# A second level of Strassen in four of the seven gate and up products

## The chip, the cores and the metric

The kernel runs on one core of a Trainium2 chip. The metric is the device time of one execution in microseconds (us), as a median of several runs. The engines are TensorE (PE in the profile; PEld is its weight loading, which has a row of its own), VectorE (DVE), ScalarE (ACT), GpSimd (POOL) and SyncE (SP), which here only issues transfers. Each engine works through its own instructions in program order, and waits where one needs what another engine has not finished.

## What is computed

A transformer block in f32, on 8 batches of 512 rows with 512 features. An attention half comes first, with a residual; the change touches it at one place only. The feed-forward half follows:

```
x = fwht(x * SU_ug) / 64                      # Hadamard transform over 512 features
x_up   = x @ W_up.T   * (Wscale_ug[:2048] * 64)
x_gate = x @ W_gate.T * (Wscale_ug[2048:] * 64)
x = silu(x_gate) * x_up                       # 2048 features
x = fwht(x * SU_dp) / 64
x = x @ W_down.T * (Wscale_dp * 64)           # back to 512
```

before it the rows are normalised, and after it they are normalised again and added to the residual. The kernel folds the second Hadamard transform into the down weights during the attention half (the tensor `wdd` in DRAM).

## The kernel before, in words

The feed-forward half is written out in program order, by hand. **Batches** are taken in four pairs, p = 0 to 3. The 2048 features are 16 blocks of 128, taken in eight **feature pairs**, i = 0 to 7: blocks i and i + 8. A **unit** (p, i, what) makes the gate ("g") or the up ("u") of one feature pair for one batch pair; the loop at the end runs through 64 of them, gate and up in turn, and its index is `u`.

A unit is a product of a weight block of 2 x 2 sub-blocks (two feature blocks by two halves of the 512 inputs) with an input of 2 x 2 (two halves of the inputs by two batches). It is done by Strassen's method (in Winograd's form) with **seven products** in place of eight. A product is two f32 matmuls of 128 x 128 weights on 512 columns, accumulated into one PSUM bank (`product`, L968). The seven are issued in the order 1, 2, 6, 5, 7, 3, 4. The weight sums S1 to S4 that they need are made by GpSimd in the first batch pair (`combine`, L146 to L149), stored to DRAM (`keep_unit`) and read back for p > 0 (`load_unit`, from SP, two units ahead). The input differences T1 to T4 are made once in each batch pair by VectorE (`operand`, L234).

`seven` takes the products out of PSUM: products 1 and 5 by a ScalarE copy (m1, m5), the others by a VectorE add onto an earlier sum. GpSimd makes c22 = u3 + m5 (L1013) and adds m5 to c12 (L1015). The last sum, u3 (L1017), is written in place: it adds product 4 to the u3 that GpSimd's c22 reads. The four results are c11, c12, u3 and c22, each 128 features by the 512 rows of a batch. `use` applies the sigmoid (ScalarE), and scales and multiplies (VectorE `scalar_tensor_tensor`, L994 for gate, L999 for up). Four PSUM banks rotate among all products (`ubank`); four others hold the sums of the down product.

`down` issues four matmuls of one feature block for the down product of one batch; it is called twice in each unit, at the filler before product 4 and after the unit, and does nothing where no block is ready. The down weights `wd` are loaded once and stay. `finish` ends a batch (scale, statistics, normalise, residual, store). `in_step` prepares a row block of the next batch pair: `in_flip` transposes it and `in_had` multiplies it by the Hadamard matrix and does the last two levels on GpSimd.

Before the loop the last batch of the attention half is finished: four times a scaling (L926), an add (L927) and a store (L928) on GpSimd. In the first unit the filler (before product 4) has the statistics of two input rows, whose shifts are on VectorE ahead of u3g.

Of the kernel before, what the change touches and what calls it, by code (L numbers as in the profile page):

```python
# [33 lines left out]
def sandwich_kernel(  # L34
# [91 lines left out]
    def load_unit(p, i, what):  # L126
        u = units.index((p, i, what))
        pool, tag = (xpool, "x") if u % 3 == 0 else (xt_p, "xT")
        t = pool.tile([P, NT, D], F32, tag=tag, name=f"w_{p}_{i}_{what}")
        w = t.rearrange("p t d -> p (t d)").rearrange("p (s k m) -> p s k m", k=2, m=P)  # L130
        wt[p, i, what] = w
        if p > 0:
            nc.sync.dma_start(
                out=w[:, 0:7].rearrange("p s k m -> p (s k m)"), in_=wsd[i, what]
            )
            return
        for h in range(2):
            nc.sync.dma_start(
                out=w[:, 2 * h : 2 * h + 2].rearrange("p s k m -> p (s k) m"),
                in_=wsrc[what][:, ts(i + h * NH, P)].rearrange("(k p) m -> p k m", p=P),  # L140
            )
# [8 lines left out]

    def keep_unit(i, what):
        wsd[i, what] = dram.tile([P, 7 * 2 * P], F32, name=f"wsd_{i}_{what}", tag=f"wsd{i}{what}")
        nc.sync.dma_start(
            out=wsd[i, what], in_=wt[0, i, what][:, 0:7].rearrange("p s k m -> p (s k m)")
        )
# [65 lines left out]
    ops = {}  # L221

    def operand(p, k):

        b11, b21 = xb[2 * p][:, 0:2], xb[2 * p][:, 2:4]
        b12, b22 = xb[2 * p + 1][:, 0:2], xb[2 * p + 1][:, 2:4]
        if k == 0:
            ops[p] = {"B11": b11, "B21": b21, "B22": b22}
        o = ops[p]
        if k % 2 == 0:  # L230
            o["home"] = qkv.tile([P, NT, D], F32, tag="v", name=f"T{k + 1}_{p}")
        o[f"T{k + 1}"] = o["home"][:, 2 * (k % 2) : 2 * (k % 2) + 2]
        a, b = [(b12, b11), (b22, o.get("T1")), (b22, b12), (b21, o.get("T2"))][k]
        nc.vector.tensor_sub(o[f"T{k + 1}"], a, b)  # L234
# [4 lines left out]
    with ExitStack() as actx:  # L239
# [684 lines left out]
        for qc in range(NT):  # L924
            y, rs, sh = ys.pop((b, qc))
            nc.gpsimd.tensor_scalar(y, y, rs[:, 0:1], sh[:, 0:1], ALU.mult, ALU.add)  # L926
            nc.gpsimd.tensor_add(y, xr[b, qc], y)  # L927
            nc.gpsimd.dma_start(out=x1d[b][ts(qc, P), :], in_=y)  # L928
# [20 lines left out]
    y0 = [fs.tile([P, D], F32, tag=f"fy{t}", name=f"fy_0_{t}") for t in range(NT)]  # L949
    r0 = [fs.tile([P, D], F32, tag=f"xres{t}", name=f"xres_0_{t}") for t in range(2)]  # L950
    psy0 = [ps_y.tile([P, D], F32, tag=f"y{t}", name=f"psy_0_{t}") for t in range(NT)]
    ubank("u0")
    wd = fw.tile([P, NI, D], F32, name="wd")

    def wd_load(i):
        for f in (i, i + NH):
            nc.sync.dma_start(out=wd[:, f, :], in_=wdd[:, ts(f, D)])
# [6 lines left out]
    def product(p, i, what, n, slot, b):  # L964
        w, rhs = wt[p, i, what], ops[p][b]
        ps = ubank(f"{what}{n}_{p}_{i}")
        for k in range(2):
            nc.tensor.matmul(  # L968
                ps, lhsT=w[:, slot, k, :], rhs=rhs[:, k, :], start=k == 0, stop=k == 1
            )  # L970
        return ps

# [8 lines left out]
    def seven(p, i, what, filler):  # L981

        def temp(n):
            return fs.tile([P, S], F32, tag=n, name=f"{n}{what}_{p}_{i}")

        def use(c, b, half):
            f = i + half * NH
            if what == "g":  # L990
                wsg = pv[:, C_WSG + f : C_WSG + f + 1]
                s = fs.tile([P, S], F32, tag="sig", name=f"s_{b}_{f}", bufs=5)
                nc.scalar.activation(s, c, AF.Sigmoid, scale=wsg)
                nc.vector.scalar_tensor_tensor(s, c, wsg, s, ALU.mult, ALU.mult)  # L994
                gs[b, f] = s
            else:
                home = free.pop(0)
                g = fs.tile([P, S], F32, tag=f"g{home}", name=f"g_{b}_{f}")
                nc.vector.scalar_tensor_tensor(  # L999
                    g, c, wsu[:, f : f + 1], gs.pop((b, f)), ALU.mult, ALU.mult  # L1000
                )
                waiting[b].append((f, g, home, now[0]))

        bA, bB = 2 * p, 2 * p + 1
        m1, m5 = temp("m1"), temp("m5")
        c11, u2, c12, u3, c22 = (temp(n) for n in ("c11", "u2", "c12", "u3", "c22"))
        nc.scalar.copy(m1, product(p, i, what, 1, A11, "B11"))  # L1007
        nc.vector.tensor_add(c11, product(p, i, what, 2, A12, "B21"), m1)
        nc.vector.tensor_add(u2, product(p, i, what, 6, S2, "T2"), m1)
        use(c11, bA, 0)  # L1010
        nc.scalar.copy(m5, product(p, i, what, 5, S1, "T1"))
        nc.vector.tensor_add(u3, product(p, i, what, 7, S3, "T3"), u2)  # L1012
        nc.gpsimd.tensor_add(c22, u3, m5)  # L1013
        nc.vector.tensor_add(c12, product(p, i, what, 3, S4, "B22"), u2)
        nc.gpsimd.tensor_add(c12, c12, m5)  # L1015
        filler()
        nc.vector.tensor_add(u3, product(p, i, what, 4, A22, "T4"), u3)  # L1017
        use(c22, bB, 1)
        use(c12, bB, 0)
        use(u3, bA, 1)  # L1020

# [3 lines left out]
    def down():  # L1025

        b = turn_of[0]
        if b == NB - 1 or not waiting[b] or waiting[b][0][3] >= now[0]:
            return
# [6 lines left out]
        for t in range(NT):  # L1036
            nc.tensor.matmul(  # L1037
                ys_[t], lhsT=g[:, ts(t, P)], rhs=wd[:, f, :], start=n == 0, stop=n == NI - 1
            )
        free.append(home)  # L1040
        psy[b] = n + 1, ys_
        if n == NI - 1:
            turn_of[0] += 1
            finish(b, ys_)

    def finish(b, ps):

        y = y0 if b == 0 else [
            fs.tile([P, D], F32, tag=f"fy{t}", name=f"fy_{b}_{t}") for t in range(NT)
        ]  # L1050
        for t in range(NT):
            nc.vector.tensor_mul(y[t], ps[t], wsdp_bc)

        def norms():
            mv = stat.tile([P, NT, 2], F32, tag="mvo", name=f"mvo_{b}", bufs=2)
            r = []
            for t in range(NT):
                r.append(
                    r0[t] if b == 0 and t < 2
                    else fs.tile([P, D], F32, tag=f"xres{t}", name=f"xres_{b}_{t}")  # L1060
                )
                nc.sync.dma_start(out=r[t], in_=x1d[b][ts(t, P), :])
                bn(mv[:, t, :], y[t], f"o{b}_{t}")
            rs = inverse_std(mv, NT, f"o{b}")

            def close():
                sh = shift_of(mv, rs, NT, f"o{b}")
                for t in range(NT):
                    nc.scalar.activation(
                        y[t], y[t], AF.Identity, bias=sh[:, t : t + 1], scale=rs[:, t : t + 1]  # L1070
                    )
                    nc.gpsimd.tensor_add(y[t], r[t], y[t])
                    nc.sync.dma_start(out=out[b, ts(t, P), :], in_=y[t])

            ends.append(close)

        ends.append(norms)
# [6 lines left out]
    CUTS = [0, 1, 2, 3, 5, 6, 8, 9, 10, 11, 12, 13, 14, 15, 16, 16, 16]  # L1084
    FIRST_CUTS = [0, 0, 1, 2, 3, 5, 6, 8, 9, 10, 11, 12, 13, 14, 15, 16, 16]
    first = 2 * NT
    wd_load(0)
    wd_load(1)
    for u, (p, i, what) in enumerate(units):
        slot = u % (2 * NH)  # L1090
        last = slot == 2 * NH - 1
        cuts = CUTS if p else FIRST_CUTS
# [3 lines left out]
        if p == 0 and u + 1 < 2 * NH:  # L1096
            combine(*units[u + 1][1:])

        def filler():
            down()  # L1100
            proceed()
            if u == 0:
                in_stats(first)
                in_stats(first + 1)
                in_shift(first)
                in_shift(first + 1)
                in_norm(first)
            if 0 < u < 4:
                wd_load(2 * u)
                wd_load(2 * u + 1)  # L1110
            if p + 1 < NP:
                for s in range(cuts[slot], cuts[slot + 1]):
                    in_step(2 * NT * (p + 1) + s // 2, s % 2, len(rows))
                if last:
                    operand(p + 1, 0)
                    operand(p + 1, 1)

        seven(p, i, what, filler)
        if p == 0:
            keep_unit(i, what)  # L1120
        if last and p + 1 < NP:
            operand(p + 1, 2)
            operand(p + 1, 3)
        down()


    b = NB - 1
    blocks = [(f, g) for f, g, _, _ in waiting[b]]

    def down_rows(ps, t, lo, hi):  # L1130
        for n in range(lo, hi):
            f, g = blocks[n]
            nc.tensor.matmul(  # L1133
                ps, lhsT=g[:, ts(t, P)], rhs=wd[:, f, :], start=n == 0, stop=n == NI - 1
            )

    def end_rows(ps, t, eng):
        y = fs.tile([P, D], F32, tag=f"fy{t}", name=f"fy_{b}_{t}")
# [18 lines left out]
    for t in range(NT):  # L1157
        rest.append(fs.tile([P, D], F32, tag=f"xres{t}", name=f"xres_{b}_{t}"))
# [71 lines left out]
```

## Time and profile before

| | us |
|---|---|
| median of three runs | 2205.27 |
| lowest and highest | 2205.2, 2208.29 |
| the profiled execution | 2205.19 |
| its span, from the first to the last instruction | 2203.4 |
| first product of the feed-forward half | at 945.97 |

The granted TensorE clock is 0.997 of full speed on average over the span. Busy time by stretch (us of the span):

| stretch | PE | DVE | ACT | POOL | PE clock |
|---|---|---|---|---|---|
| 960 to 970 | 5.80 | 3.91 | 3.12 | 9.34 | 0.79 |
| 970 to 980 | 10.00 | 7.44 | 1.88 | 4.71 | 0.87 |
| 1200 to 1300 | 100.00 | 49.28 | 20.52 | 33.76 | 1.00 |
| 1500 to 1600 | 100.00 | 48.15 | 18.24 | 30.11 | 1.00 |
| 1900 to 2000 | 100.00 | 31.70 | 14.26 | 13.96 | 1.00 |

A page of the profile gives busy time by engine, the span in 40 equal slices, the chain of work that ended last, and the groups of instructions. In a group or timeline row, "out<-in" are the tiles by the program's names, then their shapes; the bracket is the idle time of the engine before it and who ended it. An f32 matmul shows as two passes, each with its weight load. Matmul passes overlap in the records, so the mean length of one is longer than the distance from one to the next.

### The profile page before, as it was taken

What the parts mean: (1) busy time and instruction counts of PE and PEld (TensorE: products, weight loads), DVE (VectorE), ACT (ScalarE), POOL (GpSimd) and SP (SyncE); (2) the same over time, 40 slices, a digit from 0 to 9 for tenths busy, and PEclk for the clock granted to TensorE, in tenths of its full rate; (3) what the DMA queues carried; (4) which work ended last, traced back from release to release, by engine and by line L of the source; (5) the groups of instructions that cost most, each with busy time, mean ns of one, the idle gap of its engine ahead of it and who ended that gap; (6) DMA issues with size and microseconds to landing.
All of it is one profiled execution on the core that took longest, in us unless ns stands there. A gap on an engine that the chain in (4) does not pass through costs nothing.

```text
span 2203.4 us, 22074 instructions
## 1 busy us (share of the span) xinstructions
PE 2151.6 (98%) x7993; PEld 868.4 (39%) x8000; DVE 1196.7 (54%) x1659; ACT 690.5 (31%) x958; POOL 1108.5 (50%) x1161
## 2 busy tenths in 40 slices
PE   8999999999999999989999999999999999999998
PEld 3323333333333332334444444444444444444443
DVE  5687768686868676365445533534434435334322
ACT  3444555555555545522211211211211211212101
POOL 4686978787878789655544332321422311212102
PEclk9999999999999999999999999999999999999999
DMA  3112111121212022343233211212212111211201
GB/s 116 39 21 59 44 44 54 40 58 40 59 40 58 21 73 62 94 139 129 88 105 115 98 43 55 98 55 74 78 39 74 70 50 69 70 46 68 78 0 58
DMA packets 141005, 144.40 MB, mean 66 GB/s; under 512 B 83152, under 2 KB 100688, under 8 KB 140896
## 3 DMA queue, kind: packets, MB, share of 16 engines
q1 hardware_dynamic: 140544, 141.91, 20.7%
q8 instruction: 63, 1.03, 0.2%
q0 software_dynamic: 352, 1.08, 0.1%
q14 instruction: 46, 0.38, 0.1%
HBM read 106.79 MB, written 35.91 MB: 65 GB/s over the span
## 4 chain that ended last, share of the span: by engine, by line
PE 78%; POOL 9%; DVE 8%; issue 2%; ACT 2%; DMA 1%; SPq 0%; POOLq 0%; DVEq 0%; ACTq 0%
PE psy L1037 17%; PE u L968 17%; PE g L968 17%; POOL p L576 4%; PE s L513 3%; PE ps_y L643 3%; PE t L559 3%; PE ops L588 3%; DVE nm L521 3%; PE psz L1133 2%; PE ps_k L424 2%; PE t L550 1%; PE ps_cq L392 1%; PE fxh L209 1%; POOL y L675 1%
## 5 line engine op out<-in xcount | busy, mean ns | idle before, releaser
L521 DVE TENSOR_REDUCE nm<-s 128x2 f32<-128x1024 f32 x256 | 300.8, 1217 | 206.9 <-PE s L513 206.8
L1037 PE MATMUL psy<-wd,g 128*128 128x512 f32 x896 | 402.6, 592 | 0.0
L576 POOL TENSOR_TENSOR p<-p,p 128x512 f32<-128x512 f32 x244 | 325.7, 1365 | 27.0 <-PE ops L588 19.3
L570 ACT ACTIVATE p<-t 128x1024 f32<-128x1024 f32 x256 | 248.2, 1021 | 104.0 <-PE t L559 104.0
L1037 PEld LDWEIGHTS psy<-wd,g 128*128 128x128 f32 x896 | 170.2, 190 | 214.3 <-issue 214.3
L968 PE MATMUL u<-T,w_u 128*128 128x512 f32 x512 | 232.9, 598 | 4.2 <-DVE u3g L1017 4.2
L968 PE MATMUL g<-T,w_g 128*128 128x512 f32 x512 | 230.2, 592 | 0.0
L1013 POOL TENSOR_TENSOR c22u<-u3u,m5u 128x512 f32<-128x512 f32 x32 | 40.6, 1268 | 369.0 <-DVE u3u L1012 369.0
L1013 POOL TENSOR_TENSOR c22g<-u3g,m5g 128x512 f32<-128x512 f32 x32 | 40.6, 1268 | 315.2 <-DVE u3g L1012 315.1
L968 PE MATMUL g<-xb,w_g 128*128 128x512 f32 x384 | 175.3, 592 | 1.2 <-issue 1.2
L968 PE MATMUL u<-xb,w_u 128*128 128x512 f32 x384 | 175.2, 592 | 0.0
L513 PE MATMUL s<-kT,qT 32*128 32x512 f32 x1024 | 156.9, 640 | 1.6 <-DVE nm L521 1.6
L968 PEld LDWEIGHTS u<-T,w_u 128*128 128x128 f32 x512 | 97.5, 192 | 124.7 <-issue 118.2
L559 PE MATMUL t<-qT,kT 32*128 32x512 f32 x1024 | 142.9, 597 | 0.0
L968 PEld LDWEIGHTS g<-T,w_g 128*128 128x128 f32 x512 | 96.3, 190 | 116.2 <-issue 114.1
L588 PE MATMUL ops<-p,v 128*32 128x512 f32 x1024 | 136.8, 605 | 0.0
L424 PE MATMUL ps_k<-xT,wkr_sb 128*128 128x512 f32 x256 | 118.9, 608 | 0.8
L643 PE MATMUL ps_y<-wo_sb,oT 128*128 128x512 f32 x256 | 115.8, 593 | 1.0 <-DVE oT L638 0.6
L968 PEld LDWEIGHTS g<-xb,w_g 128*128 128x128 f32 x384 | 72.9, 190 | 93.4 <-issue 90.5
L968 PEld LDWEIGHTS u<-xb,w_u 128*128 128x128 f32 x384 | 73.0, 190 | 91.8 <-issue 88.7
L1007 ACT COPY m1g<-g 128x512 f32<-128x512 f32 x32 | 18.8, 586 | 254.2 <-PE g L968 217.6
L550 PE MATMUL t<-brow,ones_b 32*128 32x512 bf16 x512 | 68.5, 383 | 12.3 <-DVE nm L521 9.7
(181 smaller groups left out, 2842.9 us busy)
## 6 DMA issues: line engine op xcount, KB each, us to landing
w_g<-wsd_g SPq DMA_DIRECT2D x24, 896.0 KB, 4.5
w_u<-wsd_u SPq DMA_DIRECT2D x24, 896.0 KB, 4.6
xr<-in_x SPq DMA_DIRECT2D x32, 256.0 KB, 2.7
xin<-x1d SPq DMA_DIRECT2D x32, 256.0 KB, 2.8
xres<-x1d SPq DMA_DIRECT2D x32, 256.0 KB, 5.5
out<-fy SPq DMA_DIRECT2D x32, 256.0 KB, 2.2
rec<-rd SPq DMA_DIRECT2D x124, 64.0 KB, 2.0
x<-in_x SPq DMA_DIRECT2D x7, 1024.0 KB, 5.4
```

Source lines behind the costliest of these rows:

```text
L424: nc.tensor.matmul(ps, lhsT=wkr_sb[:, k, ts(g, P)], rhs=xT[b][:, k, :], start=(k == 0), stop=(k == NK - 1),)
L513: nc.tensor.matmul(sp[j // 2][:, j % 2, :], lhsT=qT[b][rows, g, ts(qc, P)], rhs=kT[b][rows, g, :], start=True, stop=True,)
L521: nc.vector.tensor_reduce(nms[n][:, qc, 2 * h : 2 * h + 2], sp[h], AX.X, ALU.max, negate=True)
L550: nc.tensor.matmul(sp[j // 2][:, j % 2, :], lhsT=ones_b[rows, :], rhs=brow[n][rows].rearrange("p t q -> p (t q)"), start=True, stop=False,)
L559: nc.tensor.matmul(sp[j // 2][:, j % 2, :], lhsT=kT[b][rows, g, ts(c, P)], rhs=qT[b][rows, g, :], start=False, stop=True,)
L570: nc.scalar.activation(pt[n, c, h], sp[h], AF.Exp)
L576: nc.gpsimd.tensor_add(into, into, pt[n, c, j // 2][:, j % 2, :])
L588: nc.tensor.matmul(o_ps[n][j * DH : (j + 1) * DH, :], lhsT=vv[b][:, c, ds(g * P + j * DH, DH)], rhs=pt[n, c, j // 2][:, j % 2, :], start=( ...
L643: nc.tensor.matmul(ps, lhsT=oT[b][:, k, ts(qc, P)], rhs=wo_sb[:, k, :], start=False, stop=(k == NK - 1),)
L968: nc.tensor.matmul(ps, lhsT=w[:, slot, k, :], rhs=rhs[:, k, :], start=k == 0, stop=k == 1)
L1013: nc.gpsimd.tensor_add(c22, u3, m5)
L1037: nc.tensor.matmul(ys_[t], lhsT=g[:, ts(t, P)], rhs=wd[:, f, :], start=n == 0, stop=n == NI - 1)
```

## The change

Four of the seven products, 1, 5, 7 and 3, are now made for gate and up together. The gate's and the up's two matmuls of such a product are again a 2 x 2 by 2 x 2 block product: (gate, up) by the two halves of K in the weights, the two halves of K by the two halves of the 512 columns in the input. `deep` does it with seven matmuls of 128 x 128 weights on 256 columns, each into a bank of its own. This holds for i > 0 in the second batch pair and for all i in the third and fourth (`deep_pair`), 23 feature pairs in all; products 2, 6 and 4 stay as they were. The gate unit makes the four deep products, and the up unit finds its parts of them ready in `held` (tiles h1, h5, h7, h3):

```diff
+    def deep(p, i, n, gate, up, parts):
...
+        lhs = {
+            1: wg[:, slot, 0], 2: wg[:, slot, 1], 6: s[:, 1], 5: s[:, 0],
+            7: wu[:, slot, 0], 3: s[:, 2], 4: wu[:, slot, 1],
+        }
+        rhs = {
+            1: x_[:, 0, :HS], 2: x_[:, 1, :HS], 6: t[:, 1], 5: t[:, 0],
+            7: x_[:, 0, HS:], 3: x_[:, 1, HS:], 4: t[:, 2],
+        }
...
+        m1, m5, u2, u3 = (temp(m) for m in ("m1", "m5", "u2", "u3"))
+        nc.scalar.copy(m1, small(1))
+        nc.vector.tensor_add(gate[:, :HS], small(2), m1)
+        part()
+        nc.vector.tensor_add(u2, small(6), m1)
+        nc.scalar.copy(m5, small(5))
+        part()
+        nc.vector.tensor_add(u3, small(7), u2)
+        nc.gpsimd.tensor_add(up[:, HS:], u3, m5)
+        nc.vector.tensor_add(gate[:, HS:], small(3), u2)
+        nc.gpsimd.tensor_add(gate[:, HS:], gate[:, HS:], m5)
+        part()
+        nc.vector.tensor_add(up[:, :HS], small(4), u3)
+        while parts:
+            part()
```

A `part` is one of the four matmuls of a down product, put between the small ones of deep products 1, 5 and 3 (3 only for i > 0); deep product 7 has none. In a deep unit the sums of the upper level are arranged so:

```diff
+        m1 = get(1, "m1", down_parts() if what == "g" else ())
+        if what == "g":
+            catch_up()
+        nc.vector.tensor_add(c11, product(p, i, what, 2), m1)
...
+        scaling = use(c11, bA, 0)
+        early()
+        m5 = get(5, "m5", down_parts() if what == "g" else ())
+        nc.vector.tensor_add(u2, product(p, i, what, 6), m1)
+        scaling()
+        u3 = get(7, "u3")
+        nc.gpsimd.tensor_add(u3, u3, u2)
         nc.gpsimd.tensor_add(c22, u3, m5)
+        nc.gpsimd.tensor_add(m5, m5, u2)
+        middle()
+        c12 = get(3, "c12", down_parts() if what == "g" and i > 0 else ())
         nc.gpsimd.tensor_add(c12, c12, m5)
         filler()
+        nc.vector.tensor_add(u3, product(p, i, what, 4), u3)
+        hook(4)
+        late.append(use(c22, bB, 1))
+        late.append(use(c12, bB, 0))
+        late.append(use(u3, bA, 1))
```

`early` and `middle` hold the steps of the next batch pair's rows and the ends of a batch; `catch_up` issues the scalings that the unit before left in `late`. Units that are not deep keep their seven products, but put three of their scalings off in the same way.

What the deep products need:

```diff
+    def deep_operand(p, n):
+        tt[p, n] = fs.tile([P, 3, HS], F32, tag=f"tt{n}", name=f"tt{n}_{p}")
+        x_, t = ops[p][DEEP[n]], tt[p, n]
+        nc.vector.tensor_sub(t[:, 0], x_[:, 0, HS:], x_[:, 0, :HS])
+        nc.vector.tensor_sub(t[:, 1], x_[:, 1, HS:], t[:, 0])
+        nc.vector.tensor_sub(t[:, 2], x_[:, 1, :HS], t[:, 1])
+    def deep_last(p, n):
+        x_ = ops[p][DEEP[n]]
+        nc.vector.tensor_sub(x_[:, 0, HS:], x_[:, 1, HS:], x_[:, 0, HS:])
+    def deep_weights(i):
...
+        nc.vector.tensor_add(t[:, 0], wu[:, 0:8:2, 0], wu[:, 0:8:2, 1])
+        nc.vector.tensor_sub(s3[i], wg[:, 0:8:2, 0], wu[:, 0:8:2, 0])
+        nc.vector.tensor_sub(t[:, 1], t[:, 0], wg[:, 0:8:2, 0])
+        nc.vector.tensor_sub(t[:, 2], wg[:, 0:8:2, 1], t[:, 1])
+    def deep_load(p, i):
+        w2[i] = fs.tile([P, 3, 4, P], F32, tag="w2", name=f"w2_{p}_{i}")
+        nc.sync.dma_start(out=w2[i].rearrange("p a b m -> p (a b m)"), in_=w2d[i])
```

The weight sums of the second level, `w2`, are made by VectorE in the gate units of the first batch pair, stored, and read back in one buffer at each up unit before a deep pair, behind the load of the up weights on SP. The stored up weights hold the fourth sum `s3` in place of one of their parts; feature pair 0 keeps its plain up weights too ("raw"), since p = 1, i = 0 is not deep.

To make room, the down weights no longer stay: each down product reads a tile of 256 KB, four of which rotate, loaded from `wdd` after the down product that set its buffer free. The last batch's are loaded into buffers of inputs and weights that are done with. `finish` is cut into four steps in place of two, with two residual tiles.

At the start, the four scalings of the last attention rows go from GpSimd to VectorE, and the statistics of two input rows from the first unit to the second:

```diff
-            nc.gpsimd.tensor_scalar(y, y, rs[:, 0:1], sh[:, 0:1], ALU.mult, ALU.add)
+            nc.vector.tensor_scalar(y, y, rs[:, 0:1], sh[:, 0:1], ALU.mult, ALU.add)
...
-            if u == 0:
+        def middle():
+            if u == 1:
                 in_stats(first)
                 in_stats(first + 1)
...
+        if u == 1:
+            in_shift(first)
+            in_shift(first + 1)
+            in_norm(first)
```

## Prediction

> **What bounds the kernel now.** I read four views in this order: the page's busy rows and its slices, the groups of instructions kept apart by shape, the timeline of the stretch in which the feed-forward half starts, and a close timeline of TensorE. The page first:
>
> ```profile
> PE 2151.6 (98%) x7993; PEld 868.4 (39%) x8000; DVE 1196.7 (54%) x1659; ACT 690.5 (31%) x958; POOL 1108.5 (50%) x1161
> PE   8999999999999999989999999999999999999998
> PEld 3323333333333332334444444444444444444443
> DVE  5687768686868676365445533534434435334322
> POOL 4686978787878789655544332321422311212102
> PEclk9999999999999999999999999999999999999999
> ```
>
> From slice 18 on (the span is 2203.4 us, a slice 55 us) TensorE is full, at full clock, while VectorE is at three to five tenths and GpSimd falls from five to one or two. In the last three whole stretches of 100 us (1800 to 2100) TensorE is busy for 100.00 of each, VectorE for 44.9, 31.7 and 38.5, GpSimd for 21.0, 14.0 and 18.8. So the second half is a stream of matmuls, and its length is the number of passes times the pitch of a pass.
>
> The pitch cannot be taken from the mean in the group rows (592 ns), since passes overlap. It is in the close timeline (start, us, engine, line):
>
> ```profile
> 1531.29 0.19 PEld L1037 LDWEIGHTS psy<-wd,g 128*128 128x128 f32 x1 [0.24 <-issue]
> 1531.72 0.14 PEld L200 LDWEIGHTS fxt<-ident,xin 128*128 128x128 f32 x1 [0.24 <-issue]
> 1532.15 0.60 PE L200 MATMUL fxt<-ident,xin 128*128 128x128 f32 x4
> 1532.15 0.36 PEld L200 LDWEIGHTS fxt<-ident,xin 128*128 128x128 f32 x3 [0.29 <-issue]
> 1532.48 0.30 PEld L968 LDWEIGHTS g<-T,w_g 128*128 128x128 f32 x2
> 1532.58 1.88 PE L968 MATMUL g<-T,w_g 128*128 128x512 f32 x4
> ```
>
> Weight loads in front of 512-column passes start every 0.43 us. At the start of the half, 12 passes that begin at 949.48 are followed by the next group at 954.63: 5.15 us, so a pass is 0.4292 us, and an f32 matmul, which is two passes, 0.858 us. The same lines show the short end: four transposes of 128 columns in 0.60 us, the last of them 0.273 long, are 0.109 us apart, although each has a weight load of 0.14 us; and two ordinary weight loads (0.19 us each) fit into 0.30 us.
>
> The third thing is the start of the feed-forward half:
>
> ```profile
> 958.06 3.60 PE L968 MATMUL u<-xb,w_u 128*128 128x512 f32 x8
> 961.50 1.88 PE L968 MATMUL u<-T,w_u 128*128 128x512 f32 x4
> 967.58 4.64 PE L968 MATMUL u<-T,w_u 128*128 128x512 f32 x5 [4.20 <-DVE u3g L1017]
> ```
>
> TensorE waits 4.20 us for a PSUM bank, and its granted clock then falls to 0.79 and 0.87 in the next two stretches of 10 us: the chain gives 7.87 us to 12 passes from 967.58 that need 5.15 at full clock. This place costs 4.20 + 2.72 = 6.9 us.
>
> **Removed and added on TensorE.** In 23 of the 32 feature pairs (7 of the second batch pair, 8 each of the third and fourth) the products 1, 5, 7 and 3 of gate and up, four f32 matmuls of 512 columns, become seven of 256 columns. Before: 4 x 0.858 = 3.434 us. A 256-column pass is in no row. Lower end: half of 0.4292 is 0.2146 us; with the fixed 2.5 ns of each pass that the page named below gives, 0.2158. Upper end: the weight load sets the pitch, 0.19 us plus a hand-over that no row shows; with 0.05 us it is 0.24. The transposes, 0.109 us apart under loads of 0.14, and the two loads of 0.19 in 0.30 say that loads follow each other at about 0.11 us, so I take 0.2158. Seven small matmuls are then 14 x 0.2158 = 3.02 us, 0.41 us less, and 92 products give **-38.0 us** (at 0.24: -7 us).
>
> Here a rule speaks against the change. The Trainium skill, "TensorE: Matmul & The Clock Gate", section on packing small matmuls, says that a weight load overlaps with running matmuls only where their row groups differ. All loads here use all 128 rows. By the rule a product would cost 8 x (0.429 + 0.19) = 4.95 us before and 14 x (0.216 + 0.19) = 5.68 after, and 92 of them +67 us. The row decides: 896 loads of 0.19 us of the down products stand under passes that come every 0.429 us. The load lies beside the pass before it, and 0.19 is still less than 0.216.
>
> **VectorE, ScalarE, GpSimd.** A small product leaves PSUM by a half-width add or copy. From 692 ns for 512 elements (L1014) and 1217 ns for 1024 (L521) a 256-element one is about 0.43 us (estimate), a ScalarE copy about 0.37 (0.586 for 512, 1.021 for 1024). A deep pair has on VectorE 20 half adds (8.6 us) and 6 whole ones (4.2) where 10 whole ones were (6.9); with eight scalings of 0.74 to 1.02 us (6.9 in all) it rises from 13.8 to 19.7 us. GpSimd had four adds of 1.27 (5.1 us) and gets eight of these and eight half adds of 0.73 (16 us, and 3.4 more where an input row is transformed). TensorE needs for such a pair 28 x 0.858 - 1.65 + 3.5 x 4 x 0.858 = 34.4 us. All fits beside it.
>
> The order within it matters more. The added waits are for banks: four rotate, and each small product fills half of one, so that they turn twice as fast. Deep product 7 is the tightest, since no down product lies between its parts. Counted from the end of product 6: its sum starts on VectorE 0.26 us later (the lag between the last column and the reader in the trace) and ends at 0.95, the scaling that is queued next at 1.7 to 1.9, the first half add at 2.05 to 2.35, and part 6 of 7 wants that bank at 2.15. So 0 to 0.2 us a pair. In the up unit the last sum waits until GpSimd has read its operand: product 6 ends at 3.4, GpSimd is through with two adds at about 8.3 (9.4 with an input row in front of it), and product 4 ends at 8.6 (9.5). Behind that sum on VectorE stand the first adds of the next gate unit, and TensorE has 2.2 us of banks in hand. It just fits.
>
> A second rule bears on this: the Trainium skill, "SBUF — State Buffer", section on the two sides of ports, has VectorE instructions with two SBUF inputs and GpSimd's exclude each other for whole instructions. The row agrees in part: the scaling of c12u behind GpSimd's add has a median of 1.21 us, that of c11u 0.744, so a collision costs about 0.46. By the rule each of eight scalings could wait out a GpSimd add of 1.27, +10 us a pair and VectorE at 30 of 34.4 us; by the row +3.7 us and 23. I take the row. It adds a little to the waits above.
>
> At the turn to the next batch pair the operand differences (1.22 us each), the twelve half-width ones and the four last ones come in bursts on VectorE; the banks lend about 2 us, and I count 1 to 1.5 us twice. I put all stalls of this part at **+4 us** (0 to 15).
>
> **Transfers, all on SP.** The down weights come by 112 loads of 256 KB (2.2 to 5 us to land in the trace for that size, three down products of lead, over 20 us): hidden. The weight sums (768 KB) have one buffer, free when deep product 3 is done, and stand on SP behind the next up weights (896 KB, 4.6 us), which wait for the end of the gate unit. Both have landed some 7.5 us after it (estimate: 4.6 us and 0.79 MB at the 270 GB/s that follow from 896 KB in 4.6 us and 256 KB, the stores to out, in 2.2). The third part of the next deep product 1 wants the sums 1.72 + 1.72 + 3.43 + 1.72 + 1.72 = 10.3 us after it. Hidden by 2.8 us; without that cover, 23 times the lateness. In the first batch pair VectorE makes the sums (four adds of 0.61 to 1.2 us beside a pair of 36 us) and SP stores them: covered by the down products and product 4, 5.2 us.
>
> **The start.** The chain there is GpSimd: four times a scaling (0.77), an add (1.27) and an issue (0.6 and gaps) up to 962.15, then c22g and c12g, then the inverse deviations of two input rows, whose shifts stand on VectorE in front of u3g. The change takes the scalings to VectorE (four of about 0.6 us, in front of c11g, whose bank is wanted 2 us later), and the two rows' statistics to the next unit. GpSimd then ends c22g about 961, u3g about 961.7 (962.5 behind the four weight-sum adds), and TensorE wants the bank at 963.2. The scalings now stand behind the sums of the next unit; product 4 of the up unit may wait 0.4 us for u2u. **-6.4 us** (0 to -6.9).
>
> **Sum.** Of the profiled execution's 2205.19 us (span 2203.4; the median of the runs is 2205.27): -38.0 - 6.4 + 4 = -40.4, that is 2165 us. The tail, 10 us from the last matmul to the last store, stays.
>
> **The rivals.**
> 1. VectorE and GpSimd in lock, or the weight sums' transfer, cost 0.5 to 1.2 us more in every deep pair: +12 to +28 us, 2177 to 2193. For it: GpSimd's work triples, and three places above fit by less than 1 us or hang on one queue. Against it: none of these engines is busy for over 70% of the pair.
> 2. Weight loads set the pitch of half passes at 0.24 us: -7 - 6.4 + 4, 2196 us. The transposes speak against it.
> 3. Slower: the same mechanism in the small products with a pitch above 0.25 us, from which on seven halves with the start's gain cost what four wholes do. At 0.28 (load 0.19 and 0.09 for the hand-over) a product is 3.92 us, +45 us in all, 2205 + 45 - 6 + 4 = 2248 us. Against it: the 0.109 us of the transposes, in which a load of 0.14 was not waited out.
> 4. Fewer stalls than I count, none at all: 2160 to 2161 us. It belongs to the forecast's own range.
>
> That the change does not happen can be left out: the changed program issues 644 matmuls of 256 columns in place of 368 of 512.
>
> **How the numbers follow.** Forecast (2158 to 2174) 0.64; rival 1 0.22; rival 2 0.06; rival 3 0.05; between them and no change 0.03. The range 2157 to 2185 takes the forecast and the lower half of rival 1. A measurement can tell 0.2%, 4.4 us, from no change: faster 0.93, same 0.02, slower 0.05.
>
> **What would show it.** Weight loads of L1071 0.216 us apart (right) or 0.24 and more (rivals 2, 3). TensorE solid from 946 to the end with no wait of over 0.5 us in the deep pairs; waits of L1071 on the half adds, or of the sums on GpSimd, each of 23 pairs, are rival 1. No 4.2 us gap near 963 and a clock of 1.00 there. It would be wrong if a wait turned up in the first batch pair, whose order changes too.

## The result, and the profile after

The changed kernel takes 2174.26 us (median of four runs, 2172.91 to 2177.87) against 2206.78 for the kernel before on the same chip: a ratio of 0.9855, with a 95% interval of 0.9838 to 0.9872. The profiled execution took 2173.1 us, 32.1 less than the one before; the forecast was 40 less. One profile further down fell in a slower state of the chip, at a granted clock of 0.946 (2242.51 us): no stretch is read from it, and that kernel was run a second time.

The page of the changed kernel, busy rows and slices:

```profile
span 2171.3 us, 24623 instructions
PE 2115.1 (97%) x8552; PEld 971.1 (45%) x8552; DVE 1360.4 (63%) x2111; ACT 701.9 (32%) x1050; POOL 1352.1 (62%) x1433
PE   7999999999999999999999999999999999999998
DVE  6686768686868676465655755657555557455432
POOL 4686878787878879754554266464565644444542
PEclk9999999999999999999999999999999999999999
```

TensorE stays full from slice 17 on, with less to do. VectorE is mostly at five to seven tenths there, GpSimd at four to six. The small products are the rows of L1071, read here in the close timeline of an undisturbed stretch of the fourth batch pair, with a row of their weight loads (PEld) from one of the third (start, us, engine, line):

```profile
1971.50 1.88 PE L1050 MATMUL g<-T,w_g 128*128 128x512 f32 x4
1973.21 1.03 PE L1071 MATMUL d<-T,w_g 128*128 128x256 f32 x4
1974.08 1.03 PE L1071 MATMUL d<-tt,w 128*128 128x256 f32 x4
1974.94 0.38 PE L1071 MATMUL d<-T,w_u 128*128 128x256 f32 x1
...
1560.91 0.84 PEld L1071 LDWEIGHTS d<-tt,w 128*128 128x128 f32 x4
```

Four passes of 512 columns take 1.71 us (1971.50 to 1973.21), eight of 256 take 1.73 (1973.21 to 1974.94): 0.216 us a pass. Four weight loads of 0.19 us take 0.84 us from the start of the first to the end of the last, so they start 0.217 us apart, at the pace of the passes.

**A measure for the feed-forward half.** Programs with the same attention half reach their first feed-forward product anywhere between 944.65 and 950.31 us (more on this in the last section), so the profiles are compared from that product to the end of the last matmul pass. It lies 7.3 us before the end of the span in all of them; the sums below take 7.4 throughout, which shifts every half by 0.1 us and changes no difference. Before: 2203.4 - 7.4 - 945.97 = 1250.0 us. After: 2171.3 - 7.4 - 944.75 = 1219.1 us. The change saves 30.9 us there; the other 1.2 us of the profiled executions lie ahead of it.

**Where TensorE still waits.** I went through its timeline and took, for each group of passes, the distance to the next group less its passes times their pitch. These are the places of 0.25 us and more: the start of the half (2.96 us), the first unit of the second batch pair (0.87), and the two turns to the third and the fourth pair (4.25 and 5.13 us). Then come two waits for the load of the weight sums (0.46 and 0.30), and seven gaps of 0.36 us (0.25 and 0.11) in deep products 7 and 3. Of the 5.13 us of the second turn, 1.7 are no wait: behind its first wait the granted clock is 0.50 from 1813.25 to 1816.66. The start and the first turn in TensorE's timeline:

```profile
964.95 3.70 PE L1050 MATMUL u<-T,w_u 128*128 128x512 f32 x8 [2.80 <-DVE u3g L1169]
...
1507.26 0.70 PE L1071 MATMUL d<-xb,w_u 128*128 128x256 f32 x2 [2.74 <-DVE h L1193]
...
1514.73 1.12 PE L1217 MATMUL psy<-wd,g 128*128 128x512 f32 x2 [1.18 <-DVE g L1142]
```

The bracket says who ended the wait: the last sum of a unit (u3g, or h in the up unit), which frees a PSUM bank, and a scaling whose result is a down product's weight. What held the first two is in VectorE's timeline, first ahead of u3g, then ahead of h; two rows of GpSimd's stand behind it, the first and the last of its four sums at the turn:

```profile
955.93 2.06 DVE L991 TENSOR_TENSOR w<-w_u 128x512 f32<-128x512 f32 x1
957.91 4.13 DVE L992 TENSOR_TENSOR s<-w_g,w_u 128x512 f32<-128x512 f32 x1
961.96 1.21 DVE L993 TENSOR_TENSOR w<-w,w_g 128x512 f32<-128x512 f32 x1
963.20 1.09 DVE L994 TENSOR_TENSOR w<-w_g,w 128x512 f32<-128x512 f32 x1
964.22 0.68 DVE L1169 TENSOR_TENSOR u3g<-g,u3g 128x512 f32<-128x512 f32 x1
...
1499.44 0.42 DVE L976 TENSOR_TENSOR tt<-T 128x256 f32<-128x256 f32 x1
1499.89 1.37 DVE L977 TENSOR_TENSOR tt<-T,tt 128x256 f32<-128x256 f32 x1
1501.29 1.37 DVE L978 TENSOR_TENSOR tt<-T,tt 128x256 f32<-128x256 f32 x1
1502.59 1.48 DVE L976 TENSOR_TENSOR tt<-T 128x256 f32<-128x256 f32 x1
1504.10 1.37 DVE L977 TENSOR_TENSOR tt<-T,tt 128x256 f32<-128x256 f32 x1
1505.51 0.42 DVE L978 TENSOR_TENSOR tt<-T,tt 128x256 f32<-128x256 f32 x1
1505.85 0.42 DVE L983 TENSOR_TENSOR xb<-xb 128x256 f32<-128x256 f32 x1
1506.18 0.42 DVE L983 TENSOR_TENSOR T<-T 128x256 f32<-128x256 f32 x1
1506.52 0.68 DVE L1193 TENSOR_TENSOR h<-u,h 128x512 f32<-128x512 f32 x1
...
1498.94 2.04 POOL L1186 TENSOR_TENSOR h<-h,u2u 128x512 f32<-128x512 f32 x1 [5.70 <-DVE u2u L1183]
1503.86 1.32 POOL L1191 TENSOR_TENSOR h<-h,h 128x512 f32<-128x512 f32 x1
```

The same instruction takes 0.42 us or 1.37. From 1498.94 to 1505.18 GpSimd does the four sums of the up unit; each stretched difference ends 0.28 or 0.29 us after one of them (1501.26 after 1500.98, 1505.47 after 1505.18), so it looks like waiting for the sum to end. At 956.15 to 961.48 GpSimd adds a residual row, then c22g, c12g and the first weight sum of the next unit. The four sums of L991 to L994 take 8.5 us.

### The profile page after: what moved, and what is told of

Its sections match the earlier page's. It is cut to its first block, busy times and chain, and to the rows that moved or that the text cites. A ratio compares the mean times of both kernels' runs of the same rounds, so it can differ in the third digit from the quotient of the medians.

```text
span 2171.3 us, 24623 instructions
## 1 busy us (share of the span) xinstructions
PE 2115.1 (97%) x8552; PEld 971.1 (45%) x8552; DVE 1360.4 (63%) x2111; ACT 701.9 (32%) x1050; POOL 1352.1 (62%) x1433
## 4 chain that ended last, share of the span: by engine, by line
PE 74%; DVE 10%; POOL 9%; issue 3%; DMA 2%; ACT 2%; POOLq 0%; SPq 0%; DVEq 0%; ACTq 0%
PE psy L1217 17%; PE d L1071 12%; PE g L1050 10%; PE u L1050 9%; POOL p L590 4%; PE s L527 3%; DVE nm L535 3%; PE ps_y L657 3%; PE t L573 3%; PE ops L602 3%; PE psz L1379 3%; PE ps_k L438 2%; PE ps_cq L406 1%; PE t L564 1%; DVE p L595 1%
## 5 line engine op out<-in xcount | busy, mean ns | idle before, releaser
L1091 POOL TENSOR_TENSOR h<-du,dm 128x256 f32<-128x256 f32 x92 | 66.8, 726 | 251.0 <-DVE du L1090 237.7
L1050 PE MATMUL u<-T,w_u 128*128 128x512 f32 x328 | 151.5, 592 | 2.8 <-DVE u3g L1169 2.8
L1050 PE MATMUL g<-T,w_g 128*128 128x512 f32 x328 | 151.3, 592 | 0.7 <-DVE T L248 0.7
L1050 PEld LDWEIGHTS u<-T,w_u 128*128 128x128 f32 x328 | 61.8, 190 | 78.7 <-issue 73.2
L1071 PE MATMUL d<-tt,w 128*128 128x256 f32 x368 | 94.6, 380 | 0.4 <-DMA w<-w2d 0.3
L1050 PE MATMUL g<-xb,w_g 128*128 128x512 f32 x200 | 92.6, 592 | 1.2 <-issue 1.2
L1050 PE MATMUL u<-xb,w_u 128*128 128x512 f32 x200 | 92.5, 592 | 0.0
L1090 DVE TENSOR_TENSOR du<-d,du 128x256 f32<-128x256 f32 x92 | 39.1, 425 | 80.1 <-PE d L1071 76.6
L1071 PEld LDWEIGHTS d<-tt,w 128*128 128x128 f32 x368 | 69.6, 190 | 39.3 <-issue 27.0
L527 PEld LDWEIGHTS s<-kT,qT 32*128 32x128 f32 x1024 | 48.4, 183 | 78.0 <-issue 48.6
```

The costliest lines, as they stand in the source:

```text
L527: nc.tensor.matmul(sp[j // 2][:, j % 2, :], lhsT=qT[b][rows, g, ts(qc, P)], rhs=kT[b][rows, g, :], start=True, stop=True,)
L1050: nc.tensor.matmul(ps, lhsT=w[:, SLOT[n], k, :], rhs=rhs[:, k, :], start=k == 0, stop=k == 1)
L1071: nc.tensor.matmul(ps, lhsT=lhs[m], rhs=rhs[m], start=True, stop=True)
L1091: nc.gpsimd.tensor_add(up[:, HS:], u3, m5)
```

## The experiments

My theory: the deep products bring what the pass counts say, and some 13 us are lost again where VectorE's instructions with two SBUF inputs meet GpSimd's, ahead of a sum that holds a bank. The rivals: part of the gain is of the new order; the stalls come from the amount of work on VectorE, not from its meeting GpSimd.

**No deep pair.**

```diff
     def deep_pair(p, i):
-        return p > 1 or p == 1 and i > 0
+        return False
```

(and the half-width operands of the second batch pair left out)

> No feature pair is deep: all units keep their seven products of 512 columns. The new order, the streamed down weights, the weight sums made and stored in the first batch pair and the moved scalings stay. My theory: the 92 deep products save 0.43 us each on TensorE (39.5 us) and give back about 10 us at the two turns between batch pairs, so this kernel is 29 to 31 us slower than the changed one, 2202 to 2206 us, that is 3 to 5 us below before from the start alone. Rival: a good part of the gain is of the new order and the put-off scalings; then 2180 to 2195 us.

Measured: 2200.91 us, ratio 0.9975 (0.9966 to 0.9984), feed-forward half 2201.5 - 7.4 - 950.31 = 1243.8 us. So all that is not deep brings 6.2 us (1250.0 to 1243.8), and the deep products 24.7 net. The time is a little below my 2202 to 2206; a part of the gain that I hadn't counted is of the order: before, TensorE waited in three places for xflat in front of a Hadamard product, 0.87 or 0.88 us each, and here it doesn't. The 2.79 us wait at the start is here too, so it has nothing to do with deep products.

**The differences ahead.** In the last up unit of a batch pair, those of deep products 5 and 7:

```diff
         def early():
+            if last and p + 1 < NP:
+                deep_operand(p + 1, 5)
+                deep_operand(p + 1, 7)
+                deep_last(p + 1, 1)
+                deep_last(p + 1, 7)
             if steps:
```

(in place of the same lines ahead of the last sum)

> In the last up unit of a batch pair the half-width operand differences of deep products 5 and 7 and two of the four last ones go ahead of u2u on VectorE, where GpSimd has nothing to do, instead of ahead of the last sum. My theory: the differences take 1.4 us each because GpSimd adds at the same time, and the last sum behind them holds a PSUM bank; here they take 0.42 us, and the waits of 2.74 and 2.75 us go, with the slow clock after the second: 6 to 8 us less than the changed kernel, 2166 to 2168 us in the profiled run. Rival: the burst is only moved; u2u and GpSimd's sums behind it come 2 us later and the last sum waits for them: within 1 us of 2173.

Measured: 2172.33 us, ratio 0.9851 (0.9836 to 0.9866), half 1216.8 us. At the turn where the changed kernel has the rows shown above, the differences take 0.41 to 0.43 us, and the 2.74 us wait has become 0.34. But two others stand beside it: 0.81 us for the scaling of c11u, now behind the differences, and, at the two turns, 1.43 and 1.86 us for the late scalings, behind the burst of the next unit (1.18 at the first turn of the changed kernel). The two turns together lose 7.0 us in place of 9.4. In the half that is 2.3 us of 6 to 8. Half a miss: the cause is right, the place chosen gave part of it back.

**The first pair's weight sums later.**

```diff
-            if p == 0 and what == "g":
+            if p == 0 and what == "g" and i > 0:
                 deep_weights(i)
...
+        if u == 0:
+            deep_weights(0)
```

> The weight sums of feature pair 0 (four VectorE instructions) are issued after the first unit instead of ahead of its last sum u3g. My theory: TensorE's 2.80 us wait near 962 is for u3g, which stands behind them (8.5 us, stretched by GpSimd's adds); the wait goes or falls under 0.5 us, and the run is 2.3 to 2.9 us shorter, about 2170.5 us in the profiled run. Rival: GpSimd's c22g, which u3g must wait for, or c11u behind the moved sums takes the wait's place: no change.

Measured: 2175.36 us, ratio 0.9862 (0.9847 to 0.9877), half 1218.2 us. The 2.80 us wait is gone; in its place TensorE waits 0.50 for c11u and 0.60 for u2u. A gain of 0.9 us in the half where 2.3 to 2.9 was expected, which the runs' times can't tell from none. The gaps at the start alone fall from 2.96 to 1.43 us; the turns of this profile lose 0.5 us more than those of the changed kernel, with the stretch of half clock at the first turn instead of the second.

**Less work for GpSimd at the turn.**

```diff
+        whole = not (what == "u" and i == NH - 1 and p in (1, 2))
+        if whole:
+            nc.gpsimd.tensor_add(m5, m5, u2)
...
+        if whole:
+            nc.gpsimd.tensor_add(c12, c12, m5)
```

> Leaves out two of GpSimd's four sums in the last up unit of the second and the third batch pair (m5 + u2 and c12 + m5), so one of four results of that unit lacks two summands; VectorE's order is that of the changed kernel. If GpSimd's adds stretch the differences: those that start once GpSimd is idle (the last three of six) take 0.42 us, and each of the two waits of 2.7 us falls to 0.7 to 1.2. If they are slow by themselves or the burst is what counts: 1.37 us each, and waits of 2.7 us.

Measured: half 1215.7 us (one run, 2170.89 us), and the two waits are 0.73 and 0.72 us. VectorE's timeline of this kernel, the same instructions in the same order:

```profile
1502.22 0.42 DVE L976 TENSOR_TENSOR tt<-T 128x256 f32<-128x256 f32 x1
1502.67 1.37 DVE L977 TENSOR_TENSOR tt<-T,tt 128x256 f32<-128x256 f32 x1
1504.07 1.38 DVE L978 TENSOR_TENSOR tt<-T,tt 128x256 f32<-128x256 f32 x1
1505.37 0.41 DVE L976 TENSOR_TENSOR tt<-T 128x256 f32<-128x256 f32 x1
1505.81 0.43 DVE L977 TENSOR_TENSOR tt<-T,tt 128x256 f32<-128x256 f32 x1
1506.28 0.42 DVE L978 TENSOR_TENSOR tt<-T,tt 128x256 f32<-128x256 f32 x1
```

and GpSimd's:

```profile
1501.72 2.04 POOL L1186 TENSOR_TENSOR h<-h,u2u 128x512 f32<-128x512 f32 x1 [5.68 <-DVE u2u L1183]
1503.83 1.33 POOL L1187 TENSOR_TENSOR c22u<-h,h 128x512 f32<-128x512 f32 x1
```

The first difference meets GpSimd's first add and comes through in 0.42 us; there it is GpSimd that pays: its add takes 2.04 us where 1.27 is usual. The next two take 1.37 while GpSimd adds, until 1505.16; the fourth starts after that and takes 0.41. VectorE has the same work in the same order, so it is the meeting that costs. It makes the longer wait of each turn, for h, but not the one behind it: for the late scalings TensorE still waits 1.17 and 1.61 us.

**The bursts spread.** The differences of 5 behind those of 3 in the last gate unit, those of 7 on GpSimd, T4 and a last one into `middle` of the new pair's first gate unit:

```diff
+                    deep_operand(p + 1, 7, nc.gpsimd)
+                    deep_last(p + 1, 7, nc.gpsimd)
...
+            if two and slot == 0:
+                operand(p, 3)
+                deep_last(p, 3)
```

> The bursts at the turns between batch pairs are spread: the differences of deep product 5 go behind those of 3 in the last gate unit, those of 7 and its last one to GpSimd behind its sums, T4 and two last ones of the new pair behind c11g. My theory (VectorE's queue stretched by GpSimd's adds makes all of the waits at the turns): of the 9.4 us that TensorE loses at the two turns 1 to 3 are left, the feed-forward half takes 1211 to 1213 us against 1219.1, and the ratio to before is 0.981 to 0.983. Rival (the sums of the turn are too many for VectorE in any order, as the second experiment's new waits of 0.8 and 1.4 to 1.9 us suggest): 5 us or more are left, 1215 us or more.

Measured: 2180.48 us, ratio 0.9886 (0.9872 to 0.9901), half 1221.5 us: worse than the changed kernel. There are five waits at the first turn and four at the second, the longest 1.33 us (for the first half add of deep product 1) and 1.80 (for a last difference in `middle`). Both stand behind a difference that met GpSimd: T2 takes 1.78 us beside the up unit's sums, T4 and the last one in `middle` 1.61 and 1.48 beside GpSimd's sums for deep product 7 and u3g. I had put these two where GpSimd is busiest. By its numbers this one speaks for the rival; the fastest kernel below decides.

**The first pair's weight sums on GpSimd**, behind c12g:

```diff
+        if u == 0:
+            deep_weights(0, nc.gpsimd)
```

> The four weight sums of feature pair 0 are made by GpSimd behind c12g instead of by VectorE. If they hold u3g and then c11u only by standing ahead of them on VectorE, the 2.80 us wait near 962 goes and none comes in its place: feed-forward half 1216 us or a little more against 1219.1. Rival: GpSimd's later sums of unit 1's weights or c22u come late and TensorE waits up to 3 us in units 1 and 2.

Measured: 2173.94 us, ratio 0.9856 (0.9841 to 0.987), half 1218.1 us. One wait of 1.21 us, for u2u, is left: the scalings ahead of it on VectorE take 1.75, 1.75 and 1.21 us beside GpSimd's new sums, where 0.74 is usual. The gaps at the start fall from 2.96 to 1.37 us; at the turns this profile loses 0.9 us more than the changed kernel's, with half clock behind both waits for h instead of one. Between the two expectations.

**Both, and the weight sums' load first on SP.**

> Both of these, and the load of the second level's weight sums ahead of the up weights on SP. My theory adds them up: 6.5 to 8.5 us of the turns, 2.8 of the start, 0.5 of the two waits for that load: feed-forward half 1207 to 1210 us, ratio to before 0.979 to 0.982. If the losses move elsewhere: 1212 us or more.

Measured: 2177.84 us, ratio 0.9875 (0.9858 to 0.9891), half 1221.0 us. With the spread bursts in it, it falls with them. Four of the seven profiles with the changed kernel's order of loads show waits of TensorE for the weight sums (up to 0.63 us in the bracket). Counted by gaps, all seven lose something ahead of the small products that read these sums, 0.16 to 0.79 us at the worst place; this one loses nothing there, nor do the later kernels with the load first. So the order of the loads does it, and it is worth less than 1 us.

**The changed kernel again.**

> The changed kernel once more, on the same chip as these: ratio 0.984 to 0.987, feed-forward half within 1.5 us of 1219.1, waits of 2.7 us at both turns.

Measured: 2176.81 us, ratio 0.9871 (0.9856 to 0.9886), half 1219.7 us, waits of 2.75 and 2.74 us at the turns. As expected, with the ratio at the edge.

**The bursts where GpSimd is idle.**

```diff
                 deep_operand(p + 1, 3)
+                deep_operand(p + 1, 5)
...
+            if last and p + 1 < NP:
+                deep_operand(p + 1, 7)
+                deep_last(p + 1, 1)
+                deep_last(p + 1, 7)
+            if slot == 0:
+                deep_last(p, 5)
             if steps:
                 in_step(*steps.pop(0))
+            if slot == 0:
+                operand(p, 3)
+                deep_last(p, 3)
```

(the first line stands in the last gate unit behind product 4, the next four in the last up unit ahead of u2u, the others in the first gate unit behind c11g; with the first pair's weight sums after the first unit, and the load of weight sums first on SP)

> The bursts placed once more, this time where GpSimd is idle: the differences of deep product 5 in the last gate unit, those of 7 and two last ones ahead of u2u in the last up unit, T4 and two last ones behind c11g in the first gate unit; the weight sums of pair 0 after the first unit, and their load first on SP. If what counts is that VectorE's instructions with two SBUF inputs meet no GpSimd add: losses of 2 to 4 us at both turns together in place of 9.4, feed-forward half 1209 to 1213 us. If VectorE has too much to do at the turn in any order: 6 us or more lost there, 1215 us or more.

Measured: 2168.31 us, ratio 0.9825 (0.9811 to 0.9838). The stretches are read from its second run:

> The kernel with the bursts where GpSimd is idle, once more, for a profile at full clock: losses of 2 to 4 us at both turns together, at the start about 1 us, feed-forward half 1209 to 1213 us (1215 or more if VectorE has too much to do at the turn in any order), ratio to before 0.981 to 0.984.

Measured: 2167.01 us, ratio 0.9823 (0.981 to 0.9836), half 2165.5 - 7.4 - 946.73 = 1211.4 us. TensorE's timeline at the turn (the brackets in its second and fourth lines are all that is left of the waits), and VectorE's row of h:

```profile
1501.50 1.03 PE L1071 MATMUL d<-xb,w_g 128*128 128x256 f32 x4
1503.35 1.12 PE L1217 MATMUL psy<-wd,g 128*128 128x512 f32 x2 [0.82 <-DVE g L1142]
1505.17 1.02 PE L1217 MATMUL psy<-wd,g 128*128 128x512 f32 x2
1506.54 0.70 PE L1071 MATMUL d<-xb,w_u 128*128 128x256 f32 x2 [0.35 <-DVE h L1193]
...
1505.80 0.69 DVE L1193 TENSOR_TENSOR h<-u,h 128x512 f32<-128x512 f32 x1 [2.50 <-POOL c22u L1187]
```

Each turn loses 1.7 us in place of 4.25 and 5.13, and no stretch of half clock falls into this half. VectorE has as much to do at the turns as before. The rival falls: it is the place, not the amount. What is left of the wait for h is no longer VectorE's queue: VectorE sits idle for 2.50 us there, until GpSimd has made c22u. The start loses 1.46 us, where about 1 was expected. Against the kernel before, this one is faster by 38 and 40 us in the medians of its two runs; its ratios of 0.9825 and 0.9823 stand against 0.9855 and 0.9871 of the changed kernel.

**The second and third experiment together, with the load first.**

> The second and the third experiment together, with the load of the weight sums first on SP. If their gains in the feed-forward half (2.4 and 1.0 us) add, and the load's waits (about 0.7 us) go: 1214.5 to 1216 us against 1219.1; if they do not, 1217 us or more.

Measured: 2174.2 us, ratio 0.9852 (0.9837 to 0.9867), half 2172.2 - 7.4 - 948.13 = 1216.7 us. Between the two by its sum, and no better than the second experiment alone (1216.8). The gaps show why: the start loses 1.46 us in place of 2.97, and the waits for the load are gone, but the granted clock is 0.50 from 1821.19 to 1824.59, behind the wait of 1.87 us at the second turn. That costs 1.5 us, and the second experiment's profile has no such stretch. So the gain of the later weight sums is there, and the sum hides it.

## Why the prediction was right, and where its size was off

The time lies within the range of 2157 to 2185 us, 9 us above the forecast of 2165. The mechanism was right, and the passes brought what was forecast; two other terms were off, and one was not seen. Term by term, in the feed-forward half:

| term of the sum | predicted, us | measured, us |
|---|---|---|
| passes of 92 deep products | -38.0 | -37.5 |
| start of the half | -6.4 | -4.0 |
| waits for xflat, and for T2 in the second pair | not seen | -2.2 |
| stalls around the deep products | +4 | +12.8 |
| sum | -40.4 | -30.9 |

The third column: 92 times 3.434 less 14 x 0.2162 (the 14 small and 8 wide passes from 1965.04 to 1971.50 take 6.46 us); 6.9 less 2.96; the 6.2 us of the kernel without deep pairs less that 4.0; and what is then left of the deep products' 24.7 net. The gaps listed above, without the start and the 0.87, come to 12.7, so little of the 12.8 is left unplaced.

- **The passes** were right: seven small matmuls at 0.216 us a pass are 3.03 us, against 3.43. The weight loads, 0.19 us each, stay hidden under passes of 0.216, with all row groups in use. So the rule on row groups from the Trainium skill ("TensorE: Matmul & The Clock Gate", section on packing small matmuls), as the prediction quotes it, doesn't hold for these loads. The same section names a second way, which the prediction left out: a load into the background weight buffer is also pulled ahead of running matmuls. The rows above agree with that. Rivals 2 and 3 are out.
- **The start** was half right. Moving the four scalings and the two rows' statistics brought c22g to an end at 959.57 (forecast 961), and in this profile the slow clock went. What I took at 962.5 came at 964.9: the four weight-sum adds ahead of u3g, priced at 0.61 to 1.2 us, took 8.5 us. So 2.96 of the 6.9 us stayed; 4.0 were gained, 1.4 of them by the shorter wait and 2.6 because no slow clock followed. The second part is not sure: of six profiles with this wait of 2.8 us, one (the fourth experiment's) has a granted clock of 0.50 for 3.4 us behind it and loses 1.4 us. The prediction had named a wait in the first batch pair as a sign of being wrong, and this is one.
- **The failing term is the stalls**, +4 us. The single places in a deep pair were judged rightly: outside the turns the losses are a few gaps of 0.36 us and two waits of 0.46 and 0.30. "I count 1 to 1.5 us twice" for the turns is what was wrong: 4.25 and 5.13, together 9.4, by the list above (7.7 of waits and 1.7 of half clock). I had counted the differences of a turn by their lengths alone (0.42 is what a half-width one takes) and asked how far the banks reach; beside GpSimd's four sums they take 1.4 us. The fourth experiment shows this for the waits for h. For the waits for the late scalings, the meeting is not shown to be the cause: T4 and a last difference ahead of them take 1.38 and 0.94 us beside one of GpSimd's sums, where 1.21 and 0.42 are usual, but the fastest kernel, where these waits are gone, moves both behind c11g.
- **The rule that I set aside was the better guide** for this. By the Trainium skill, "SBUF — State Buffer", section on the two sides of ports, a VectorE instruction with two SBUF inputs and one of GpSimd exclude each other for whole instructions. I took the row of before (0.46 us a collision) since that is what its scalings showed, one GpSimd add at a time. Here it is 0.95 us a collision (1.37 - 0.42), and one instruction (4.13 us) stood through three adds in a row, which a wait for one whole instruction does not explain. What the rule spares holds too: half adds that read PSUM and SBUF take 0.41 to 0.43 us, whatever GpSimd does. The scalings, put off into the next unit, came out better than I had allowed for: medians of 0.74 in gate units and deep up units.
- **The weight sums' load** was hidden, as said; it lands in 6.1 us (5.8 to 8.6). The cover is thinner than my 2.8 us: in all seven profiles with this order TensorE loses something to it, 0.16 to 0.79 us at the worst place.
- **Not seen at all**: the waits for xflat, 3.1 us, were in the kernel before and are gone in the new order; a wait of 0.87 for T2 came. That the two together took 2.2 us off the miss is luck.

Rival 1 (0.5 to 1.2 us more in every deep pair) is not what happened, though its time was near: the pairs are clean, and two turns and the start hold the loss.

## What to carry to other kernels

Trading large matmuls for more small ones pays here as the pass counts say, with weight loads of 0.19 us under passes of 0.216; no run tried a shorter pass with such a load. Of the elementwise work that comes with it, price each instruction with two SBUF inputs by what GpSimd does at that moment, not by its length alone, and put bursts of such instructions where GpSimd is idle. Look first at the seams of a loop (its start, the turn to the next block), where one-off work stands in a queue ahead of a sum that frees a bank.

## What the runs showed of the hardware that was not expected

- VectorE and GpSimd stretch each other by more than one instruction: 4.13 us for a weight sum that takes 0.68 to 1.76 in the seven later pairs, 2.04 for a GpSimd add of 1.27.
- The first feed-forward product comes at 944.65 to 950.31 us in programs whose attention half is the same. The two earliest profiles have a granted clock of 1.00 in the first 60 us, the four that come at 949.5 and later 0.91, and these four also have 3.4 us at 0.50 near 832 us. That is 5 us of 2170, as much as some of the effects here, so a difference of a few us had to be read from the half itself.
- A wait of TensorE can be followed by a slower clock. In the profiles at full clock it has one form wherever it comes ahead of the last matmul: the granted clock is 0.50 for 3.41 us, or for twice that, and 1.00 before and behind it. One stretch of 3.41 us in the feed-forward half cost 1.4 to 1.8 us of matmuls. It came behind the 2.75 us wait at 1809 of the changed kernel and not behind the same wait at 1504; in the third experiment it was the other way round, and in the sixth it came behind both. What decides it stays open.
- So the halves differ by such stretches too: none falls into those of the second experiment and of the fastest kernel, two into those of the sixth and seventh, one into the others with deep pairs. At a turn part of the loss is won back, since a wait further on is then shorter: the second turn of the changed kernel loses 5.13 us with such a stretch, that of the third experiment 4.7 without one.
